# Softmax denominators: an early and a late division for the last sequence, and reciprocals cut in four

## The chip, the cores and the metric

The kernel runs on one core of one Trainium2 chip. The metric is device time in microseconds (us) for one execution; the time of a version is the median of several runs. Before the change it is 2147.88 us (three runs, 2146.33 to 2148.32).

## What is computed

Four layers act in turn on two sequences of 1024 tokens with 512 features, each on a layer-normalised input and each added to its input: a gated recurrence, a feed-forward block with ternary weights, a causal attention, and the same feed-forward block again. The change lies in the attention. Cut to what matters:

```python
q = jnp.concatenate([q1, q2], axis=1)        # two query sets, 16 heads of 32 each
scores = jnp.einsum('bhqd,bhkd->bhqk', q, repeat(k, 2)) * scale
p = jax.nn.softmax(where(causal, scores, min), axis=-1)
y = jnp.einsum('bhqk,bhkd->bhqd', p, repeat(v, 2))
y1, y2 = (y[:, :H], y[:, H:])
y = y1 - sigmoid(x @ Wlam) * y2              # per token and head
out = y.reshape(B, T, D) @ Wo
```

So each of the 32 query heads has a softmax denominator per token. The second set is also weighted by lambda before it is subtracted.

## The kernel before

**Staging.** Each layer keeps its tokens in on-chip memory (`xres`, 16 tiles of 128 tokens). In the attention, a sequence has 16 "pairs": a pair is two heads of one query set that are worked together, and the 32 pairs of both sequences (`pairs`, tuples of sequence `b`, group `g`, position `p`, parity `par`) run one after the other. Each pair has six steps. A step computes two blocks of transposed scores (`weights_step`: `t` products at L866 and L874, exponentials on ScalarE at L882, a causal select on GpSimd at L885 for diagonal blocks), the row maxima of the *next* pair (`maxima_step`: `s` products at L805, reductions on VectorE at L815 and L820), and the products with the values of the *previous* step (`weigh`, L904).

**Numerators and denominators.** The values carry a column of ones, so each product `y` holds 32 rows of numerators and one row of denominators per head. `qb` is the half of the sequence (512 queries). When a half of a pair is complete, ScalarE copies `y` to `ys` (L921) and four transfers on SyncE's queue bring it to its place: two to `share` (L924, the numerators) and two to `tot` (L929, one row of denominators each). `tot` is one tile of 48 rows by 1024 tokens for a sequence: rows 0 to 15 for the first query set, rows 32 to 47 for the second; it is filled with 1.0 first (L917).

**Division.** `divide(b, e)` works on half `e` of `tot`, in place. VectorE takes the reciprocal (L937), multiplies the second set's rows by lambda (L939), and splits the result into a rounded part (L943) and the rest (L944) in a tile `factors`, which GpSimd has cleared (L941). `combine(b, c, e)` spreads the factors of one quarter `c` of the features over the partitions with two products (`r`, L951), multiplies the shares by them on VectorE (L954), and subtracts the second share from the first on GpSimd (L955). `project_out(b, j)` multiplies 128 tokens with `Wo` (L965: eight instructions of TensorE) and VectorE adds the result to the residual (L970). A token tile needs all four quarters of its half. The 16 rows of denominators of quarter `c` come from the four pairs whose `2 * (g % 2) + par` is `c`; for `c = 3` the last of them is the very last pair.

**Order.** TensorE's order in this layer is the program's (`manual_schedule` for PE). The order of the other engines, and of SyncE's queue, is made by the framework's planner, which works with its own idea of costs. In the end part VectorE's order is by hand too. Work beside the pairs is hung on a pair and a step by `at(n, step, f, ...)`, and is issued after that step's `weigh`. For the first sequence, both divisions and all combines hang on pair 16, the first one of the second sequence, whose step 0 also holds the eight value projections (L702). For the second sequence, `divide(1, 0)` hangs on step 3 of the last pair (31), two combines on its step 5, and the rest follows the loop. Steps 0 to 2 of pair 31 also prepare the next layer's first input (L136, L127, L474, L475).

**Room.** All products of this layer go through a ring of seven PSUM banks (`ring_bank`); the `y` and the very last `project_out` have one bank of their own (`edge_bank`). The feed-forward layer that follows loads its 16 weight tiles (`w`, L569) into the room that this layer's tiles leave, in order, from SyncE's queue.

## Time and profile before

| what | value |
|---|---|
| median of 3 runs | 2147.88 us (2146.33 to 2148.32) |
| profiled execution, its own time | 2146.65 us |
| span of that execution, first to last instruction | 2144.9 us |
| mean granted clock of TensorE | 0.996 of full |
| attention layer, roughly | 770 to 1775 us |
| end of it: last pair's step 0 to the next layer's first product | 1720.5 to 1774.6 us |
| reciprocal of half a `tot` (48x512) | 3345 ns, 4 times |
| lambda multiply / cast / subtraction of it | 682 / 418 / 686 ns (medians) |
| `r` product, `b_out` product, `share` multiply, `share` subtraction | 397 / 592 / 682 / 1268 ns (medians) |

How to read it: the page gives busy time by engine over the whole span, but the layers have different limits, so the stretch around a division has to be looked at by itself. A timeline row has the start, the busy time, the engine, the line and the operation (out <- in), the count of instructions merged in it, and in brackets the idle time just before it with what ended it. A wait that no other engine needs is harmless. Matmul durations overlap their neighbours', so a group's length is read from start to start. Dates are us from the start of the span.

### The profile page before, as it was taken

What the parts mean: (1) busy time and instruction counts of PE and PEld (TensorE: products, weight loads), DVE (VectorE), ACT (ScalarE), POOL (GpSimd) and SP (SyncE); (2) the same over time, 40 slices, a digit from 0 to 9 for tenths busy, and PEclk for the clock granted to TensorE, in tenths of its full rate; (3) what the DMA queues carried; (4) which work ended last, traced back from release to release, by engine and by line L of the source; (5) the groups of instructions that cost most, each with busy time, mean ns of one, the idle gap of its engine ahead of it and who ended that gap; (6) DMA issues with size and microseconds to landing.
All of it is one profiled execution on the core that took longest, in us unless ns stands there. A gap on an engine that the chain in (4) does not pass through costs nothing.

```text
span 2144.9 us, 28054 instructions
## 1 busy us (share of the span) xinstructions
PE 2108.8 (98%) x10615; PEld 1242.2 (58%) x10624; DVE 1069.1 (50%) x2272; ACT 835.2 (39%) x1590; POOL 449.8 (21%) x812
## 2 busy tenths in 40 slices
PE   8999999999999999999999999999999999999998
PEld 3444444688888854444444444444545447888887
DVE  5766686533343234555555465464546662433322
ACT  4444333234344322444444422243434523333333
POOL 1312212122122221111111113021212221121212
PEclk9999999999999999999999999999999999999999
DMA  6111211600000111111110101201110033000000
GB/s 255 59 59 62 86 59 74 250 1 1 1 1 1 35 46 37 41 26 41 23 44 21 46 8 37 57 20 42 24 32 15 14 111 132 20 1 20 1 20 20
DMA packets 50999, 98.71 MB, mean 46 GB/s; under 512 B 10800, under 2 KB 19120, under 8 KB 50864
## 3 DMA queue, kind: packets, MB, share of 16 engines
q1 hardware_dynamic: 50864, 96.93, 13.8%
q8 instruction: 83, 1.36, 0.3%
q14 instruction: 52, 0.43, 0.1%
HBM read 58.75 MB, written 16.78 MB: 35 GB/s over the span
## 4 chain that ended last, share of the span: by engine, by line
PE 83%; DVE 8%; DMA 4%; ACT 2%; issue 1%; POOL 1%; SPq 1%; DVEq 0%; ACTq 0%; POOLq 0%
PE y L904 12%; PE g L524 11%; PE u L524 11%; PE f_out L545 11%; PE s L805 10%; PE pq L737 8%; PE t L866 8%; PE pv L702 3%; PE b_out L965 2%; DMA w<-in_w_pt_dram 1%; DMA w_kept<-w 1%; DVE one L174 1%; PE kv L269 1%; DVE w L179 1%; PE ag L269 1%
## 5 line engine op out<-in xcount | busy, mean ns | idle before, releaser
L882 ACT ACTIVATE pr<-t 128x512 f32<-128x512 f32 (+3 forms) x768 | 314.8, 497 | 380.6 <-PE t L874 380.4
L815 DVE CUSTOM_DVE_ANT_0 s<-s,causal 128x128 f32<-128x128 f32 (+3 forms) x512 | 245.3, 510 | 126.1 <-PE s L805 117.4
L904 PE MATMUL y<-pr,val 128*64 128x512 f32 (+3 forms) x1536 | 291.6, 501 | 0.2 <-POOL pr L885 0.2
L539 POOL TENSOR_TENSOR ssq<-ssq,sq 128x512 f32<-128x512 f32 x120 | 155.9, 1299 | 603.6 <-ACT sq L538 603.6
L530 DVE TENSOR_TENSOR h<-h,u 128x512 f32<-128x512 f32 x128 | 88.0, 688 | 362.0 <-PE u L524 355.9
L524 PE MATMUL g<-xs,w 128*128 128x512 f32 x1024 | 262.4, 398 | 0.9 <-ACT xs L474 0.7
L545 PE MATMUL f_out<-w,hs 128*128 128x512 f32 x1024 | 257.7, 394 | 0.3 <-DVE hs L533 0.3
L820 DVE TENSOR_REDUCE nmax<-s 128x1 f32<-128x512 f32 x256 | 165.0, 686 | 184.4 <-PE s L805 184.3
L524 PE MATMUL u<-xs,w 128*128 128x512 f32 x1024 | 256.4, 392 | 0.0
L805 PE MATMUL s<-gr,gr 32*128 32x512 f32 (+3 forms) x1536 | 248.8, 492 | 2.6 <-DVE nmax L815 2.6
L524 PEld LDWEIGHTS u<-xs,w 128*128 128x128 f32 x1024 | 192.4, 188 | 43.5
L545 PEld LDWEIGHTS f_out<-w,hs 128*128 128x128 f32 x1024 | 191.6, 188 | 43.9 <-DVE hs L533 1.1
L524 PEld LDWEIGHTS g<-xs,w 128*128 128x128 f32 x1024 | 190.9, 189 | 44.0 <-ACT xs L474 0.9
L866 PE MATMUL t<-gr,gr 32*128 32x512 f32 (+3 forms) x1536 | 198.8, 533 | 0.0
L904 PEld LDWEIGHTS y<-pr,val 128*64 128x64 f32 x1536 | 93.5, 136 | 179.9 <-issue 105.7
L737 PE MATMUL pq<-b_xt,w_qk 128*128 128x512 f32 x384 | 176.0, 603 | 0.0
L805 PEld LDWEIGHTS s<-gr,gr 32*128 32x128 f32 x1536 | 147.6, 185 | 46.8 <-issue 14.0
L532 ACT CAST hs<-h 128x512 fp32r<-128x512 f32 x128 | 79.4, 621 | 236.6 <-DVE h L530 236.6
L885 POOL TENSOR_SCALAR_AFFINE_SELECT pr<-pr 128x256 f32<-128x256 f32 x256 | 101.3, 408 | 332.2 <-ACT pr L882 332.2
L529 ACT ACTIVATE h<-g 128x512 f32<-128x512 f32 x128 | 76.5, 598 | 224.3 <-PE g L524 224.1
L533 DVE TENSOR_TENSOR hs<-h,hs 128x512 fp32r<-128x512 f32 x128 | 88.6, 692 | 83.1 <-ACT hs L532 83.1
L737 PEld LDWEIGHTS pq<-b_xt,w_qk 128*128 128x128 f32 x384 | 69.6, 189 | 88.0 <-issue 74.0
(155 smaller groups left out, 2211.0 us busy)
## 6 DMA issues: line engine op xcount, KB each, us to landing
w<-w_kept SPq DMA_DIRECT2D x32, 768.0 KB, 8.7
w_kept<-w SPq DMA_DIRECT2D x16, 768.0 KB, 3.2
gr<-gr SPq DMA_DIRECT2D x96, 128.0 KB, 2.3
w<-in_w_gu_dram SPq DMA_DIRECT2D x32, 256.0 KB, 2.8
share<-ys SPq DMA_DIRECT2D x128, 64.0 KB, 2.0
w_in<-in_w_in_t_dram SPq DMA_DIRECT2D x5, 1024.0 KB, 11.2
x<-in_x_dram SPq DMA_DIRECT2D x16, 256.0 KB, 7.1
w<-in_w_pt_dram SPq DMA_DIRECT2D x16, 256.0 KB, 3.5
```

Source lines behind the costliest of these rows:

```text
L524: nc.tensor.matmul(po, ws[f][:, part, ts(k, P)], xs[:, e, k, :], start=(k == 0 and e == 0), stop=(k == NKC - 1 and e == 1),)
L533: nc.vector.tensor_sub(hp[:, 1, :], h, hp[:, 0, :].bitcast(F32))
L539: nc.gpsimd.tensor_add(ssq, ssq, sq)
L545: nc.tensor.matmul(po[j], hp[:, e, ts(j, P)], ws[f][:, 2, :], start=(f == 0 and e == 0), stop=(f == NF - 1 and e == 1),)
L737: nc.tensor.matmul(po, w[:, k, ts(kind, P)], xts[b][:, k, ts(e, BLK)], start=(k == 0), stop=(k == NKC - 1),)
L805: nc.tensor.matmul(part, queries[:, ts(j, P)], keys[:, first : first + nk], start=True, stop=True,)
L815: nc.vector.tensor_tensor_reduce(part, part, causal[:, BLK - part.shape[-1] :], -1.0, 3.0e38, ALU.add, ALU.min, top,)
L820: nc.vector.tensor_reduce(top, part, AX.X, ALU.max, negate=True)
L866: nc.tensor.matmul(banks[u, e][:, :nq], keys[:, ts(kb, P)], queries[:, (qb + 1) * BLK - nq : (qb + 1) * BLK], start=True, stop=False,)
L882: nc.scalar.activation(pr[:, e, :nq], banks[u, e][:, :nq], AF.Exp)
L885: nc.gpsimd.affine_select(out=pr[:, :, :P], in_=pr[:, :, :P], compare_op=ALU.is_ge, fill=0.0, base=0, pattern=[[0, 2], [1, P]], channel_mu ...
L904: nc.tensor.matmul(y[64 * e : 64 * e + 64, lo:], all_values[:, HV * (NH * kb + h) : HV * (NH * kb + h) + 64], pr[:, e, : BLK - lo], start= ...
```

## The change

For the second sequence, the denominators are divided twice. `late_totals` runs in step 0 of the last pair: GpSimd copies `tot` as it is by then (all pairs but the last) to a tile `late_tot`, and clears a tile with room for three sets of factors. The last pair's rows go to `late_tot`. `divide(1, 0)` moves from step 3 to step 0 of that pair and works on `tot`; its factors serve three quarters, whose combines hang on steps 2 and 3. A second division of the first half works on `late_tot`, in step 3, and serves the last quarter, in step 5. The second half is divided from `tot` in step 4, and from `late_tot` in the end part; each set of factors has its own room there. The end part is reordered: `project_out(0)`, three combines of the second half, `project_out` 1 to 3, the last combine, the rest. `late_tot` takes a slot of the tag `w_qk`, the extra factors one of the tag `group0`. Reciprocals of `tot`, the first sequence's too, are taken in four pieces of 128 columns; those of `late_tot` in one.

```diff
@@ weigh
+            tot = held["late"][0] if pair == pairs[-1] else totals[b]
...
-                    out=totals[b][32 * (g // 2) + h : 32 * (g // 2) + h + 1, ts(qb, BLK)],
+                    out=tot[32 * (g // 2) + h : 32 * (g // 2) + h + 1, ts(qb, BLK)],
...
-        def divide(b, e):
-
-            part = totals[b][:, ts(e, BLK)]
-            nc.vector.reciprocal(part, part)
+        def divide(b, e, late=None, to=None):
+
+            part = (totals[b] if late is None else late)[:, ts(e, BLK)]
+            if late is None:
+
+                for i in range(NKC):
+                    nc.vector.reciprocal(part[:, ts(i, P)], part[:, ts(i, P)])
+            else:
+                nc.vector.reciprocal(part, part)
             second = part[rows_of[1]]
             nc.vector.tensor_mul(second, second, lams[b][rows_of[1], ts(e, BLK)])
-            factors[b, e] = b_c.tile([96 + NH, BLK], F32R, tag="factors", name=f"factors{b}_{e}")
-            nc.gpsimd.memset(factors[b, e].bitcast(F32), 0.0)
-            hi, lo = (factors[b, e][64 * i : 64 * i + 32 + NH] for i in range(2))
+            if to is None:
+                to = b_c.tile([96 + NH, BLK], F32R, tag="factors", name=f"factors{b}_{e}")
+                nc.gpsimd.memset(to.bitcast(F32), 0.0)
+            factors[b, e] = to
+            hi, lo = (to[64 * i : 64 * i + 32 + NH] for i in range(2))
             nc.vector.tensor_copy(hi, part)
             nc.vector.tensor_sub(lo, part, hi.bitcast(F32))
+
+        def late_totals(b):
+
+            sums = b_b.tile([32 + NH, SEQ], F32, tag="w_qk", name=f"late_tot{b}")
+            nc.gpsimd.tensor_copy(sums, totals[b])
+
+            more = b_d.tile([96 + NH, 3, BLK], F32R, tag="group0", name=f"factors{b}_late", bufs=2)
+            nc.gpsimd.memset(more.bitcast(F32), 0.0)
+            return sums, [more[:, i, :] for i in range(3)]
...
-        at(n, 3, divide, 1, 0)
-        for c in range(2):
-            at(n, 5, combine, 1, c, 0)
+
+        at(n, 0, lambda: hold("late", late_totals, 1))
+        at(n, 0, divide, 1, 0)
+        for c in range(NKC - 1):
+            at(n, 2 + c // 2, combine, 1, c, 0)
+
+        at(n, 3, lambda: divide(1, 0, held["late"][0], held["late"][1][0]))
+        at(n, 4, lambda: divide(1, 1, None, held["late"][1][1]))
+        at(n, 5, combine, 1, NKC - 1, 0)
...
-        for c in range(2, NKC):
-            combine(1, c, 0)
         ordered.enter_context(tc.manual_schedule(engines={mybir.EngineType.DVE}))
-        divide(1, 1)
-        for j in range(QB - 1):
-            project_out(1, j, held["o", 1])
-        for c in range(NKC):
-            combine(1, c, 1)
-        for j in range(QB - 1, NQ):
-
-            project_out(1, j, held["o", 1], ring_bank if j < NQ - 1 else edge_bank)
+        w_o = held["o", 1]
+        for j in range(QB):
+            project_out(1, j, w_o)
+            if j == 0:
+                for c in range(NKC - 1):
+                    combine(1, c, 1)
+                divide(1, 1, held["late"][0], held["late"][1][2])
+        combine(1, NKC - 1, 1)
+        for j in range(QB, NQ - 1):
+            project_out(1, j, w_o)
+
+        project_out(1, NQ - 1, w_o, edge_bank)
         ordered.close()
```

More of the change, by code (lines that the diff above doesn't have):

```diff
@@ L682 @@
         ]
-        groups, nmax, lams, totals, shares, factors = {}, {}, {}, {}, {}, {}
+        groups, nmax, lams, totals, shares, factors, held = {}, {}, {}, {}, {}, {}, {}
         def load_weights(b, g):
@@ L977, in at @@
             beside.setdefault((n, step), []).append((f, args))
-        held = {}
         def hold(key, f, *args):
```

## The prediction, made before the result was known

> **What bounds the kernel now.** I read the page first, then the list of waits with TensorE as the waiter, then timelines by engine around its longest waits, then the granted clock by the microsecond.

> ```profile
> PE 2108.8 (98%) x10615; PEld 1242.2 (58%) x10624; DVE 1069.1 (50%) x2272; ACT 835.2 (39%) x1590; POOL 449.8 (21%) x812
> ```

> TensorE is busy for 98% of the span. A gain has to come out of its 36 us of gaps, or out of its clock. The waits of TensorE over the whole run:

> ```profile
> PE s L805 <- DVE nmax L815: 2.6, 1, 2.6
> ...
> PE r L951 <- DVE factors L944: 1.8, 1, 1.8
> ...
> PE b_out L965 <- POOL share L955: 0.6, 1, 0.6
> ```

> These three are all that the change can remove; the other long ones lie in the first layer and at block edges. The first (VectorE's timeline, then TensorE's):

> ```profile
> 1251.86 0.14 DVE L815 DVE_READ_ACCUMULATOR2_ANT nmax<- 128x1 f32 x1
> 1252.99 3.35 DVE L937 RECIPROCAL tot<-tot 48x512 f32<-48x512 f32 x1 [0.99 <-DMA tot<-ys]
> 1256.27 0.40 DVE L815 CUSTOM_DVE_ANT_0 s<-s,causal 128x256 f32<-128x256 f32 x1
> ```

> ```profile
> 1257.54 1.51 PE L805 MATMUL s<-gr,gr 32*128 32x384 f32 x8 [2.59 <-DVE nmax L815]
> 1258.98 3.44 PE L904 MATMUL y<-pr,val 128*64 128x512 f32 x8
> ```

> VectorE runs the first sequence's division ahead of maxima whose banks TensorE wants back. TensorE stands 2.59 us, and the y group behind it takes 3.44 us where the same form took 1.94 at 1251.14. The windows say why (columns: stretch, length, PE, PEld, DVE, ACT, POOL, granted clock, DMA):

> ```profile
> 1257.50:1259.00 1.50, 1.46 (x10) 1.04 (x10) 1.43 (x4) 0.00 (x0) 1.29 (x4) 1.00 0.00 0
> ...
> 1260.00:1261.00 1.00, 1.00 (x4) 0.24 (x2) 0.98 (x2) 0.00 (x0) 0.26 (x1) 0.50 0.00 0
> ```

> After the gap the clock is halved, from 1259.3 to 1262.7. That costs 1.50 on y and 0.13 on the transposes behind it: 1.6 us. This place is worth 2.6 + 1.6 = 4.2 us.

> The last pair of heads, TensorE and then VectorE:

> ```profile
> 1729.15 0.66 PE L136 MATMUL xnt_f<-ident,xn_f 128*128 128x128 f32 x4
> 1729.74 1.14 PE L866 MATMUL t<-gr,gr 32*128 32x512 f32 x8
> ...
> 1736.84 1.73 PE L904 MATMUL y<-pr,val 128*64 128x512 f32 x8
> 1740.32 1.19 PE L951 MATMUL r<-factors,head_of 112*128 112x512 f32 x4 [1.75 <-DVE factors L944]
> ```

> ```profile
> 1734.99 3.35 DVE L937 RECIPROCAL tot<-tot 48x512 f32<-48x512 f32 x1 [2.74 <-DMA tot<-ys]
> ```

> Here the 1.75 us are those of the division that waits for this pair's own sums; the clock stays whole. Steps 0 to 2 of this pair are over by 1729.74. Keep that date.

> **The change part by part.**

> *Reciprocals in four pieces.* A 48x512 reciprocal is 3.345 us, the 128x8 one 0.203, the 128x4 ones 0.17 to 0.18 and the 128x1 one 0.136: about 6.3 ns a column and 0.13 fixed. A piece of 128 columns is then about 0.94 us, four are 3.75, 0.4 more than one. [...] I go by the rows: with one piece before the maxima, the first of the two wanted banks comes back about 0.94 + 2 x 0.38 = 1.7 us after 1253.0, at 1254.7, and TensorE asks for it at about 1254.95. The gap goes, and the half clock with it: -4.0 (leaving 0.2 of the 4.2). Bounds: -4.2, and +0.4 if the four stay together. The second reciprocal of this sequence (1273.5) lies beside value projections where VectorE waits 2.7 us for each; nothing there.

> *The early division in the last pair.* It is placed in step 0 and waits for more than it needs. The pool copy of the sums reads all of the tile, so also what pair 30 wrote last; and the reciprocal writes in place, so it waits for the copy. Dates from before: the last of those four sum and share transfers is issued at 1726.08 and lands some 1.9 later (1733.04 to 1734.99 is the nearest like it): 1728.0. Copy 48x1024 on GpSimd: not in the trace. Below: its memset of that shape, 0.97. Above: twice a two-input 128x512, 2.5. Nearest are the one-input selects, 0.41 for 256 and 0.735 for 512, which make 1.4 for 1024; I take 1.3. So 1729.3. Then four pieces 3.75, multiply 0.72, cast 0.42, subtraction 0.69: 5.6; with some of the 0.69 of an xs subtraction that comes ready at 1731.5, the factors are there at about 1735.4 (1734.7 to 1737.5). GpSimd's memsets (1536 columns, about 1.4 by the 0.95 of 1024; and 0.52) end by 1731.3, ahead of the cast. They and the copy block the queue, but nothing in it is due between 1726.1 and 1735.6.

> *Three combines moved to steps 2 and 3.* TensorE goes in program order. The first r product stands right behind the transposes at 1729.15, so it is due at 1729.74 and gets its factors at 1735.4: a new gap of 5.65 us (4.9 to 7.7). Behind it in TensorE's queue stand steps 3 to 5 and everything after. The first sequence has the same spacing of steps, but there 27.7 us of value projections lie in step 0; here nothing does. [...]

> *The late division, first half.* Sums still land at 1735.0, since the y they come from precede the new gap. VectorE then holds the four multiplies (4 x 0.68), reciprocal 3.35, 0.72, 0.42, 0.69, and two more multiplies: 9.3 us from 1735.4, to about 1744.7. TensorE reaches its combine at 1735.4 + 1.2 (four r) + 3.2 + 0.6 + 3.1 + 2.5 = 1746.0, later still at half clock. So 1.75 goes. In a bad order (the 5.6 us of the other early division first) it is up to 4 late again.

> *The second half's two divisions and the reordered end.* The early one is 5.6 us of VectorE before the combines behind project_out(0), due at about 1746.0 + 0.6 + 0.9 + 3.5 = 1751; VectorE's whole list ends at about 1735.4 + 16 = 1751.4. The late one needs about 4.2 us from the y copy to the landing (1742.39 to 1746.57 before) and 5.2 of work; it lies beside project_out 1 to 3, 3 x 3.45 = 10.4 us of TensorE. Vector additions queue behind it, whose banks are wanted much later. Only the last combine's multiplies and GpSimd subtraction (0.4 + 1.36 + 1.27 = 3.0) against six of the eight products of project_out(4) (2.6) may show 0.4. The 0.62 of before goes: project_out(0) now has the y products as well. Together I put 0.5 for waits in this order (0 to 4).

> *Room.* The copy of the sums lies in the weights' room, where a load of the next layer will land, so that load and those behind it on SP's queue wait until the late division has read. Before, five loads went at 1745.5, two at 1757.7 and nine at 1775.2. Some may slip by about 10 us; the fifth is wanted about 22 us after that layer's start (5.6 us a step). Zero, unless slips exceed 20 us.

> **Sum.** Last pair: + 5.65 + 1.6 + 0.5 - 1.75 - 0.62 = + 5.4. First sequence: - 4.0. Net about + 1.5 us (1.4, rounded). The profiled execution took 2146.65 (span 2144.9, 1.75 around it), so 2148.1; it lies 1.2 under the median 2147.88, and against that median I say 2149.4. A measurement here tells about 0.2%, 4.3 us, from no change.

> **Rivals.**

> *A, as summed*, 0.6: 2149.4, own range 2146 to 2152.5.

> *B, the pieces run back to back*, 0.25, the slower side. The planner that orders VectorE put the whole reciprocal ahead of the maxima once; if in its reckoning VectorE is idle for longer than two pieces, they still stand together, at 1253. Price: the 4.0 isn't earned and 0.4 is added, 2147.9 + 5.4 + 0.4 = 2153.7. It decides from the third piece on, when the bank is about 1.9 us late. For it: VectorE had waited 0.99 us for the sums' transfer there, so the planner believed it idle. Against: the maxima's products were done at 1251.2.

> *C, the change does both things freely*, 0.05: no new gap, and all three waits go: 4.2 + 1.75 + 0.6, some 6.5 less, 2141.4. It needs factors at 1729.74, only 1.7 after the landing, against 6.9 of work.

> *D, order on VectorE or GpSimd*, 0.1: the 3.35 us late reciprocal slips in ahead of the multiplies that free banks, or the pool copy ahead of step 1's selects (due 1725.4, 2.6 before the landing): 2 to 4 more than A, 2152.4.

> Range: 2146.0 to 2154.4, which takes in B and most of D. Faster by over 0.2%: C, 0.05. Slower: most of B, some of D and of A's upper end, 0.3. Within: 0.65.

> **What would show it.** In the profile after: 48x128 reciprocals with 0.9 each; no wait of s on nmax near 1255 and clock 1.00 there; in the last pair a wait of r for factors of about 5.6 us followed by a clock of 0.5; the late division's factors ready before their r. No such wait there would refute me, and so would four adjacent pieces at 1253.

## The result, and the profile after

The changed kernel takes 2160.92 us (four runs, 2157.49 to 2162.71) beside 2147.57 of before: 1.0061 times as long, 95% interval 1.0043 to 1.0078. The forecast was 2149.4, at most 2154.4. The profiled execution took 2162.71, span 2161.0: 16 us more than before. I place them by four marks that both traces have: the first product of the first feed-forward layer, the first value projection (`pv`) of the second sequence, the first input transpose (`xnt_f`) of the last pair, and the first product of the feed-forward layer behind the attention:

| stretch | before | after | difference |
|---|---|---|---|
| start to the first feed-forward product | 398.6 | 402.3 | +3.7 |
| from there to the first `pv`, with the first sequence's division | 870.4 | 872.4 | +1.9 |
| `pv` to the last pair's `xnt_f` | 453.8 | 454.1 | +0.4 |
| `xnt_f` to the next layer's first product ("the tail") | 51.8 | 61.9 | +10.0 |
| rest, to the last instruction | 370.3 | 370.3 | 0.0 |

Nothing in the first stretch was edited; the runs below show that it is chance. The busy times, the first line of the page after, say little: VectorE has 10 us more for 20 instructions more, and TensorE 10 us more for the same 10615 products: a product at half clock counts as busy for longer (a `y` group takes 3.44 us in the prediction's rows where 1.94 is its time at whole clock).

```profile
PE 2118.6 (98%) x10615; PEld 1246.7 (58%) x10624; DVE 1079.4 (50%) x2292; ACT 835.5 (39%) x1590; POOL 451.7 (21%) x813
```

The list of TensorE's waits over the whole run, after, tells more. Columns: who waits for whom, us in total, times, the longest.

```profile
PE r L968 <- DVE factors L952: 6.8, 1, 6.8
...
PE a_out L421 <- POOL yt L395: 2.9, 1, 2.9
...
PE y L904 <- POOL pr L885: 1.9, 2, 1.7
PE t L866 <- DVE nmax L820: 1.1, 1, 1.1
...
PE s L805 <- DVE nmax L815: 0.6, 2, 0.4
```

The 2.59 us of `s` are down to 0.6 in two waits, the 1.75 of `r` has become 6.8, and two waits are new: `t` for a maximum, and `y` for one of GpSimd's selects (1.65). (`a_out` is of the first layer.)

**First sequence.** VectorE's timeline after, then TensorE's:

```profile
1257.71 0.95 DVE L941 RECIPROCAL tot<-tot 48x128 f32<-48x128 f32 x1 [1.00 <-DMA tot<-ys]
...
1260.06 2.56 DVE L941 RECIPROCAL tot<-tot 48x128 f32<-48x128 f32 x3
1262.65 0.68 DVE L945 TENSOR_TENSOR tot<-tot,lam 16x512 f32<-16x512 f32 x1
1263.37 0.42 DVE L951 CAST factors<-tot 48x512 fp32r<-48x512 f32 x1
1263.82 0.69 DVE L952 TENSOR_TENSOR factors<-tot,factors 48x512 fp32r<-48x512 f32 x1
1264.54 0.69 DVE L820 TENSOR_REDUCE nmax<-s 128x1 f32<-128x512 f32 x1
```

```profile
1259.86 1.51 PE L805 MATMUL s<-gr,gr 32*128 32x384 f32 x8 [0.20 <-DVE nmax L815]
...
1265.29 0.37 PE L866 MATMUL t<-gr,gr 32*128 32x128 f32 x1 [1.08 <-DVE nmax L820]
...
1266.21 2.31 PE L805 MATMUL s<-gr,gr 32*128 32x512 f32 x6 [0.38 <-DVE nmax L815]
1268.44 3.11 PE L904 MATMUL y<-pr,val 128*64 128x512 f32 x8
```

One piece stands ahead of step 3's maxima, and there only 0.20 us of wait is left, as forecast. But the other three pieces, the lambda multiply, the cast and the subtraction follow in one row, 4.5 us to 1264.54, ahead of the next step's maximum. The wait has moved on by one step, and the half clock (1268.6 to 1272.1) with it: `y` takes 3.11 us, as it took 3.44 before.

**Last pair.** TensorE after, then VectorE, then GpSimd:

```profile
1735.17 0.66 PE L136 MATMUL xnt_f<-ident,xn_f 128*128 128x128 f32 x4
1742.61 2.05 PE L968 MATMUL r<-factors,head_of 112*128 112x512 f32 x4 [6.78 <-DVE factors L952]
1744.59 2.19 PE L866 MATMUL t<-gr,gr 32*128 32x512 f32 x8
...
1756.23 2.79 PE L904 MATMUL y<-pr,val 128*64 128x512 f32 x8 [1.65 <-POOL pr L885]
```

```profile
1734.93 4.19 DVE L941 RECIPROCAL tot<-tot 48x128 f32<-48x128 f32 x5 [0.27 <-POOL late_tot L957]
...
1740.81 0.94 DVE L941 RECIPROCAL tot<-tot 48x128 f32<-48x128 f32 x1
1741.78 0.68 DVE L952 TENSOR_TENSOR factors<-tot,factors 48x512 fp32r<-48x512 f32 x1
...
1746.51 3.34 DVE L943 RECIPROCAL late_tot<-late_tot 48x512 f32<-48x512 f32 x1
...
1752.69 1.29 DVE L971 TENSOR_TENSOR share<-share,r 128x512 f32<-128x512 f32 x2
```

```profile
1733.87 1.03 POOL L957 COPY late_tot<-tot 48x1024 f32<-48x1024 f32 x1 [1.72 <-DMA tot<-ys]
...
1754.06 1.76 POOL L972 TENSOR_TENSOR share<-share,share 128x512 f32<-128x512 f32 x1 [6.08 <-DVE share L971]
1755.78 1.48 POOL L885 TENSOR_SCALAR_AFFINE_SELECT pr<-pr 128x256 f32<-128x256 f32 x4
```

The reciprocal row counts five pieces, not four: the fifth, and one more at 1740.81, belong to the second half's early division and stand ahead of the factors that TensorE waits for (the run `no_slip` below takes them away). Later the 3.34 us late reciprocal and the rest of the second half's division hold the multiplies of quarter 2 until 1752.69; GpSimd's queue has the subtraction of that quarter ahead of four selects, and `y` waits for those. The clock, by windows (columns as in the prediction's):

```profile
1740.00:1742.00 2.00, 0.00 (x0) 0.00 (x0) 1.97 (x4) 0.00 (x0) 0.00 (x0) 0.50 0.01 1
...
1744.00:1746.00 2.00, 2.00 (x10) 1.05 (x12) 2.00 (x5) 0.00 (x0) 0.53 (x1) 0.50 0.00 0
...
1747.00:1748.00 1.00, 1.00 (x6) 0.40 (x8) 1.00 (x1) 1.00 (x3) 0.98 (x1) 1.00 0.00 0
...
1758.00:1760.00 2.00, 2.00 (x6) 0.50 (x2) 0.21 (x1) 0.00 (x0) 0.00 (x0) 0.50 0.00 0
```

It is halved twice, from 1739.7 to 1746.5 and from 1756.7 to 1760.2. TensorE works in the last 3.9 us of the first stretch and all 3.4 of the second. I put the loss at half of that, 3.65 us, an estimate from the eight `t` at 1744.59, which take 2.19 us where the eight at 1733.08 take 1.14. The waits are 6.78 + 1.65 + 0.45 (`b_out`) where they were 1.75 + 0.62: 6.5 more. Together 10.2, against 10.0 measured.

### The profile page after: what moved, and what is told of

The parts are those of the page before. It is cut to its first block, busy times and chain, and to the rows that moved or that the text cites. A ratio compares the mean times of both kernels' runs of the same rounds, so it can differ in the third digit from the quotient of the medians.

```text
span 2161.0 us, 28078 instructions
## 1 busy us (share of the span) xinstructions
PE 2118.6 (98%) x10615; PEld 1246.7 (58%) x10624; DVE 1079.4 (50%) x2292; ACT 835.5 (39%) x1590; POOL 451.7 (21%) x813
## 3 DMA queue, kind: packets, MB, share of 16 engines
q8 instruction: 83, 1.36, 0.3%
## 4 chain that ended last, share of the span: by engine, by line
PE 81%; DVE 10%; DMA 3%; ACT 2%; POOL 1%; issue 1%; SPq 0%; DVEq 0%; ACTq 0%; POOLq 0%
PE y L904 12%; PE g L524 11%; PE u L524 11%; PE f_out L545 11%; PE s L805 10%; PE pq L737 8%; PE t L866 8%; PE pv L702 3%; PE b_out L982 2%; DMA w<-in_w_pt_dram 2%; DMA w_kept<-w 2%; DVE one L174 1%; PE a_out L421 1%; DVE w L179 1%; PE mt L845 1%
## 5 line engine op out<-in xcount | busy, mean ns | idle before, releaser
L815 DVE CUSTOM_DVE_ANT_0 s<-s,causal 128x128 f32<-128x128 f32 (+3 forms) x512 | 245.3, 510 | 126.0 <-PE s L805 117.3
L904 PE MATMUL y<-pr,val 128*64 128x512 f32 (+3 forms) x1536 | 292.6, 502 | 1.9 <-POOL pr L885 1.9
L805 PE MATMUL s<-gr,gr 32*128 32x512 f32 (+3 forms) x1536 | 250.1, 492 | 0.6 <-DVE nmax L815 0.6
L866 PE MATMUL t<-gr,gr 32*128 32x512 f32 (+3 forms) x1536 | 201.6, 536 | 1.2 <-DVE nmax L820 1.1
L904 PEld LDWEIGHTS y<-pr,val 128*64 128x64 f32 x1536 | 93.7, 136 | 182.3 <-issue 108.7
L805 PEld LDWEIGHTS s<-gr,gr 32*128 32x128 f32 x1536 | 147.9, 185 | 46.0 <-issue 14.0
L866 PEld LDWEIGHTS t<-gr,gr 32*128 32x128 f32 x1536 | 68.6, 184 | 90.8 <-issue 54.2
```

The lines of the kernel that those rows point to most:

```text
L805: nc.tensor.matmul(part, queries[:, ts(j, P)], keys[:, first : first + nk], start=True, stop=True,)
L815: nc.vector.tensor_tensor_reduce(part, part, causal[:, BLK - part.shape[-1] :], -1.0, 3.0e38, ALU.add, ALU.min, top,)
L866: nc.tensor.matmul(banks[u, e][:, :nq], keys[:, ts(kb, P)], queries[:, (qb + 1) * BLK - nq : (qb + 1) * BLK], start=True, stop=False,)
L904: nc.tensor.matmul(y[64 * e : 64 * e + 64, lo:], all_values[:, HV * (NH * kb + h) : HV * (NH * kb + h) + 64], pr[:, e, : BLK - lo], start= ...
```

## The experiments

All times are medians; ratios are to runs of the kernel before on the same chip. "Tail" and "`pv`" are the stretches of the table above, of the profiled execution.

**The same kernel again** (`after_again`).

> The changed kernel once more. The profiled one lost 16.1 us of span: 4.5 by the end of the first layer, whose code is not touched, 1.5 at the first sequence's division, 10.1 in the last pair and the end part. Theory (the 4.5 are the luck of the clock's windows): runs of this same program differ by some us, the profile taken now may show an offset near 0 at 1200 us, and the median lies 11 to 16 above before. Rival (the 4.5 belong to the program): every run has them, the offset at 1200 us is 4.5 again and the median 15 to 16 above before.

2158.14 us, ratio 1.0045 (1.0032 to 1.0058). To the first feed-forward product it takes 397.6 us where the first profile took 402.3; tail +8.5. So the first layer's share was chance. In the 14 profiled executions of this study that first stretch runs from 396.2 to 402.3 us, with code that no version touches.

**First sequence's reciprocals in pieces, alone** (`pieces_first`).

```diff
-            nc.vector.reciprocal(part, part)
+            if b == 0:
+                for i in range(NKC):
+                    nc.vector.reciprocal(part[:, ts(i, P)], part[:, ts(i, P)])
+            else:
+                nc.vector.reciprocal(part, part)
```

> The kernel before with the first sequence's reciprocals alone in four pieces. Theory (three of the four pieces, and the rest of the division, stand ahead of the next step's maxima; the gap moves one step on and the clock still halves): 0 to +2 us against before, a wait of the t or s products of about 1.5 us near 1264, clock 0.5 behind it. Rival (the prediction's): -4.0 us, no gap.

2149.12, ratio 1.0005 (0.9996 to 1.0013): nothing gained. VectorE's order is that of the changed kernel, one piece, four maxima, three pieces and the rest. The stretch to `pv` is 0.9 us longer than before.

**Last sequence's change, alone** (`last_seq_only`: the changed kernel, with the edit above turned round: whole reciprocals for the first sequence).

> The changed kernel with the first sequence's reciprocals whole, so only the last sequence's part of the change. Theory: +10 us against before from the wait at step 2 of the last pair (6.8), its half clock (about 2 lost), a second wait for a select (1.7) with a half clock (1.7 lost), less the two old waits (2.4); the place at 1253 as before. Rival (the pieces of the first sequence or a reordering elsewhere carry part of it): under +8.

2157.54, ratio 1.0049 (1.0036 to 1.0061); to `pv` +0.1, tail +10.0. The loss is the last sequence's.

**The first sequence's loss by order alone** (`div_behind`). The whole reciprocal, not cut, is queued on VectorE behind the first copy of the value projections.

```diff
-                    at(n + 1, 1, divide, b, 0)
+                    at(n + 1, 1, divide_behind, b, 0)
...
+        def divide_behind(b, e):
+
+            with tc.issue_after(held["pv0"].ins):
+                divide(b, e)
```

> The kernel before, with the first half's division of the first sequence queued on VectorE behind the first copy of value products, in one piece. Theory (the first sequence's loss is VectorE's order alone): the 2.6 us gap at 1255 and the half clock behind it go, -4.2 us against before. Rival (the gap only moves, or the clock's loss is made up elsewhere): 0 to -2.

2141.16, ratio 0.9972 (0.9961 to 0.9983): faster, and by more than expected. VectorE's timeline of this kernel, then TensorE's:

```profile
1265.24 0.69 DVE L705 COPY val<-pv 128x512 f32<-128x512 f32 x1 [2.73 <-PE pv L702]
1265.85 3.33 DVE L941 RECIPROCAL tot<-tot 48x512 f32<-48x512 f32 x1
```

```profile
1252.13 1.02 PE L809 MATMUL s<-gr,gr 32*128 32x384 f32 x8
1253.09 1.94 PE L908 MATMUL y<-pr,val 128*64 128x512 f32 x8
```

The same `s` stand without a wait, the `y` behind them takes its 1.94 us at whole clock, and the stretch to `pv` is 5.4 us shorter.

**Combines two steps later** (`combines_later`; this run and the next three change `last_seq_only`).

```diff
-            at(n, 2 + c // 2, combine, 1, c, 0)
+            at(n, 4 + c // 2, combine, 1, c, 0)
```

> The kernel with only the last sequence changed, but its three combines of the first half hang on steps 4 and 5 of the last pair instead of 2 and 3. Theory (the loss is that the r products stand in TensorE's queue before their factors can be there): the 6.8 us wait of r for factors at step 2 goes, with its half clock, since the factors are ready about 5 us before step 4's r products; what is left is a shorter wait for the last quarter's factors or for the second half. Its last part is 5 to 9 us shorter than with the combines in steps 2 and 3, the time about 2149 to 2152. Rival (the second division of each half is too much work for VectorE in this pair, wherever the combines stand): the wait shows up again at the later combines or in the end part with nearly its size, and the time stays at 2155 to 2158.

2158.12, ratio 1.0042 (1.0029 to 1.0054); tail +8.4. The rival was right. TensorE's timeline of this kernel, then VectorE's:

```profile
1746.86 2.07 PE L968 MATMUL r<-factors_late,head_of 112*128 112x512 f32 x4 [7.68 <-DVE factors_late L952]
```

```profile
1730.55 4.19 DVE L941 RECIPROCAL tot<-tot 48x128 f32<-48x128 f32 x5 [0.28 <-POOL late_tot L957]
...
1740.58 3.35 DVE L943 RECIPROCAL late_tot<-late_tot 48x512 f32<-48x512 f32 x1
...
1746.12 0.69 DVE L952 TENSOR_TENSOR factors_late<-late_tot,factors_late 48x512 fp32r<-48x512 f32 x1
```

Three divisions (first half early and late, second half early) and one `xs` subtraction of 0.69 fill VectorE from 1730.55 to 1746.81 without a break. Whichever product asks first waits for what is left of those 16 us. No room on TensorE's side helps; the work has to start earlier, or not be done.

**No pieces ahead of the factors** (`no_slip`). The second half's early division is queued behind the first half's.

```diff
+        def second_half():
+            with tc.issue_after(held["early"].ins):
+                divide(1, 1, None, held["late"][1][1])
...
+        at(n, 4, second_half)
```

> The kernel with only the last sequence changed; the second half's early division is queued on VectorE behind the subtraction that ends the first half's early one, so its pieces can't slip in before it. Theory: the wait of r at step 2 was 6.8 us where 5.65 was worked out because two pieces of 0.94 us stood in front of the factors; without them it is about 4.9 to 5.7 us, and the time is 1 to 2.5 us less, about 2155.5. Rival (the wait is set by GpSimd's copy and clears, not by those pieces): the wait stays at 6.8 us and the time at 2157.5.

2153.11, ratio 1.0024 (1.0015 to 1.0034). TensorE's timeline of this kernel:

```profile
1738.06 2.05 PE L968 MATMUL r<-factors,head_of 112*128 112x512 f32 x4 [4.52 <-DVE factors L952]
```

The wait falls to 4.5 us, and the tail to +4.7, more than expected: the wait of `y` for the selects behind the subtraction goes too, though GpSimd's queue has the same order. (The 0.25 us of another `y` for a select, earlier in the pair, stands in the kernel before as well.) The multiplies of quarter 2 now end at 1747.36, and TensorE comes to that `y` only at 1749.8.

**The early division brought forward** (`spread`). Its pieces are written to a place of their own, so that they don't wait for GpSimd's copy, and stand behind maxima of the pair before; the second half's early division comes behind the multiplies of the last quarter.

```diff
+        at(n - 1, 3, early_piece, 0, "top")
+        at(n - 1, 4, early_piece, 1, "top")
+        for i in (2, 3):
+            at(n, 0, early_piece, i, "min")
+        at(n, 0, lambda: divide(1, 0, done=held["room"][:, SEQ:]))
...
-        at(n, 4, lambda: divide(1, 1, None, held["late"][1][1]))
...
+            with tc.issue_after(held["mul"].ins):
+                divide(1, 1, None, held["late"][1][1])
...
         at(n, 5, combine, 1, NKC - 1, 0)
+        at(n, 5, second_half)
```

> The kernel with only the last sequence changed, with the early division brought forward: it no longer waits for GpSimd's copy (its reciprocals are written to another place), and its four pieces stand one by one behind the maxima of the last steps of pair 30 and in step 0 of the last pair; the second half's early division comes after the multiplies of the last quarter. Theory (the loss is all in the wait for factors at step 2 and what follows from it): no wait of r at step 2, no half clock there; the last part is 7 to 9 us shorter than with the early division in step 0, the time 2147 to 2150, about that of before. Rival (two divisions a half cost VectorE, and so TensorE, in any place): the time stays above 2153.

2157.16, ratio 1.0045 (1.0031 to 1.0058): missed. The wait at step 2 is gone, as the theory says, but the tail is still +8.3. TensorE's waits from 1700 to 1780 us in this kernel:

```profile
PE r L972 <- DVE factors_late L956: 3.3, 1, 3.3
PE y L906 <- POOL pr L887: 2.1, 2, 1.8
```

Both come with a half clock (1742.2 to 1745.6, 1752.4 to 1759.2). The 3.3 us are those of the second half's early division. VectorE's timeline shows where it stands:

```profile
1745.11 1.28 DVE L975 TENSOR_TENSOR share<-share,r 128x512 f32<-128x512 f32 x2 [3.01 <-PE r L972]
1746.31 3.37 DVE L945 RECIPROCAL tot<-tot 48x128 f32<-48x128 f32 x4
```

It is queued behind the multiplies of the last quarter, and for these VectorE stood idle for 3.0 us until TensorE had made their `r`. So the wait comes from this place in VectorE's order. The expectation of `first_half_only` below says that there is no idle time before these `r` products; the row shows 3.0 us of it. Whether the pieces would cost nothing there was not tried.

**With the first sequence mended too** (`both_mended`: `spread` with the edit of `div_behind`).

> The kernel of the run before this one (early division of the last sequence brought forward) with, for the first sequence, its whole reciprocal queued on VectorE behind the first copy of the value projections, as in the run div_behind. Theory: the two edits add up; the first sequence's place gives some 5 to 6 us, the last part 0 to 1 us less or more than before, together about 2142 to 2144, faster than before and about as fast as div_behind alone (2141.2), so that an early and a late division bring nothing of their own. Rival (the early and late division do take the waits of 1.75 and 0.62 away once their factors are early): 1.5 to 2.5 us under div_behind, 2139.

2151.19, ratio 1.0012 (1.0005 to 1.0018): missed by as much as the run before. To `pv` 5.0 us less, tail +8.1: the two edits add up, and the last pair's still loses.

**Only the first half divided twice** (`first_half_only`). As in `spread`, but the second half is divided once, from `late_tot`, and the end part has its old order.

```diff
-        for c in range(NKC - 1):
-            at(n, 2 + c // 2, combine, 1, c, 0)
+        for c in range(2):
+            at(n, 1 + c, combine, 1, c, 0)
...
-        at(n, 5, combine, 1, NKC - 1, 0)
-        at(n, 5, second_half)
+        at(n, 5, combine, 1, 2, 0)
```

> Only the first half of the last sequence is divided twice, early (pieces behind the maxima of the pair before) and late; the second half once, as before the change, and the end part stands in the old order. Combines of quarters 0 and 1 hang on steps 1 and 2, quarter 2 on step 5, quarter 3 follows the loop; first sequence as before. Theory (an early division is free where VectorE is idle, between 1715 and 1730, and what cost 3.3 us in the run spread was the second half's early division, which has no idle time before its r products): the wait of 1.75 us for factors goes and none takes its place; from the last pair's first input transposes to the next layer's first product it is about 50.0 us, against 51.8 before and 60.1 in spread; the time is 1 to 2 us under before, about 2146.5. Rival (a division more costs time in any place): that stretch is 54 us or longer and the time over 2150.

2144.94, ratio 0.9992 (0.9984 to 1.0). Tail 49.9 us, 2.0 less than before and within 0.2 of the forecast for it, though not quite for the reason given: a wait of 0.85 us for the late factors is left, and the 0.62 us of `b_out` are gone as well. VectorE's timeline of this kernel shows the early division in the time that was idle:

```profile
1715.53 0.94 DVE L1061 RECIPROCAL late_tot<-tot 48x128 f32<-48x128 f32 x1
...
1719.13 1.75 DVE L1061 RECIPROCAL late_tot<-tot 48x128 f32<-48x128 f32 x2
...
1722.09 0.69 DVE L956 TENSOR_TENSOR factors<-late_tot,factors 48x512 fp32r<-48x512 f32 x1
```

TensorE's timeline of this kernel, at the first `r` of the last quarter:

```profile
1740.13 0.73 PE L972 MATMUL r<-factors_late,head_of 112*128 112x512 f32 x2 [0.85 <-DVE factors_late L956]
```

0.7 us are given back ahead of the tail, at four `s` products in pair 30 right behind the piece of 1715.53: they take 1.54 us where they took 1.05 before.

**Both, and the measure for it** (`first_half_both` is `first_half_only` with the edit of `div_behind`).

> The run before this one, with the first sequence's first division queued on VectorE behind the first copy of the value projections, as in div_behind. Theory: the two add up, about 2139.5, some 1.7 us under div_behind. Rival (the wait of 1.75 us is only moved on to the next wait in that pair): no difference from div_behind.

> The kernel before with only the first sequence's first division queued behind the first copy of the value projections, once more, beside the two runs above. Theory: 2141 again, 0.3% under before; the stretch from the first value projection of the second sequence to the end is as before. No rival; it is the measure for the run before it.

2139.72, ratio 0.9967 (0.9954 to 0.9979), beside 2141.29, ratio 0.9975 (0.9965 to 0.9986), of the one edit alone. The tail is 2.0 us shorter and the stretch before it 0.7 longer; the times don't tell these 1.3 us from nothing. Both versions are faster than the kernel before and than the changed one, and nearly all of it is the order of one reciprocal.

**The pieces, held apart by hand** (`pieces_held`), one behind the last maximum of each step.

```diff
-                    at(n + 1, 1, divide, b, 0)
+                    for i in range(NKC):
+                        at(n + (i == 3), (3 + i) % STEPS, first_piece, b, i)
+                    at(n + 1, 1, divide, b, 0, True)
...
+        def first_piece(b, i):
+            part = totals[b][:, ts(i, P)]
+            with tc.issue_after(held["top"].ins):
+                nc.vector.reciprocal(part, part)
```

> The kernel before with the first sequence's first reciprocal in four pieces, as in pieces_first, but each piece is queued by hand behind the last maximum of a step (steps 3, 4 and 5 of the maxima, then the first of the next pair), and the rest of the division behind the fourth. Theory (pieces help as the prediction said when one at most stands ahead of a step's maxima; in the changed kernel three and the rest of the division stood together): no wait of s for nmax over 0.5 us near 1255 to 1266, clock whole there, and 4 to 5.4 us less than before, about 2142.5. Rival (a piece ahead of the maxima or of the copy of the turned maxima is enough to hold TensorE): a wait of about 1 us with a half clock at one of the later steps, and the time at 2146 to 2149.

2142.97, ratio 0.9979 (0.9972 to 0.9985). VectorE's timeline of this kernel:

```profile
1254.42 0.94 DVE L950 RECIPROCAL tot<-tot 48x128 f32<-48x128 f32 x1
1255.74 0.69 DVE L820 TENSOR_REDUCE nmax<-s 128x1 f32<-128x512 f32 x1 [0.38 <-PE s L805]
...
1258.12 0.94 DVE L950 RECIPROCAL tot<-tot 48x128 f32<-48x128 f32 x1
...
1261.46 0.94 DVE L950 RECIPROCAL tot<-tot 48x128 f32<-48x128 f32 x1
```

No wait of TensorE is listed from 1240 to 1280, and the stretch to `pv` is 4.9 us shorter. (The tail of this profile is 1.5 us longer: there the old wait of 1.75 us was followed by a half clock, and `b_out` waits 1.0 us where it waited 0.62.) The pieces do what the prediction asked of them once their order isn't left to the planner.

## Why the prediction was wrong

The sum was +1.4 us. The medians say +13.4 and, measured again, +10.5; the two places that the sum is about make +10.9 in the first profile.

**The first sequence: -4.0 forecast, +0.9 measured.** The step that failed is "The gap goes, and the half clock with it: -4.0", worked out "with one piece before the maxima". For those maxima it held: wait 0.20, a piece 0.95 us. The sum ended there, though, and never asked where the other three pieces and the 1.8 us behind them would stand. Rival B had the right point, "from the third piece on", but put all four ahead of the same step. The table shows TensorE's time from step 3's transposed products to the next `y`, and from there to `pv`:

| kernel | to `y` | to `pv` |
|---|---|---|
| before | 5.98 | 10.06 |
| after | 3.58 | 13.38 |
| `after_again` | 3.57 | 15.02 |
| `pieces_first` | 3.58 | 13.32 |
| `pieces_held` | 2.14 | 9.13 |
| `div_behind` | 2.14 | 8.41 |

The split gave 2.4 us in the first column and lost 3.3 in the second: +0.9. That compares profiles in which the half clock lasted 3.4 us. Where it lasted 6.8, the changed kernel takes 18.6 us (`after_again`, both columns) and the whole reciprocal 16.9 to 17.2 (`combines_later`, `no_slip`, `spread`): +1.4 to +1.7. The columns also show that the place was worth 5.5 us, not 4.2. Besides the wait of 2.59 and the 1.6 of the clock there are 1.3 us more: 0.5 lie in the eight `s` behind the wait, which take 1.51 us where they take 1.02 in `div_behind`: their weight loads start at 1257.54 and 1257.92, and VectorE's last two maxima end at 1257.48 and 1257.86, so the two banks come back 0.38 us apart; the rest is not taken apart.

**The last pair, +5.4 forecast, +10.0 and +8.5 measured.** The main mechanism was right: a wait of `r` at step 2, with the date of the landing (1728.0 forecast, 1727.9 after moving the row of 1733.87 back by the 6.0 us that this pair started later) and the price of the copy (1.3, measured 1.03) nearly right. The sizes of its terms were off, and one wait stood in none of them:
- The wait, 5.65: measured 6.78. Two pieces of 0.94 us of the other early division stood ahead of the factors; I had priced such a slip for the late factors alone. Without them (`no_slip`) it is 4.5, less than 5.65 because the four pieces in a row take 3.38 us where I had 3.75, the copy is shorter, and the `xs` subtraction falls behind the factors; and the whole tail is then +4.7, beside the +5.4 of the sum. That this is so near is in part luck: the shorter wait is made up for by a half clock of 6.8 us (1737.3 to 1744.1), twice as long as the one that the 1.6 was read from.
- The half clock, 1.6: that is the price read at the 2.59 us wait of the first sequence; that a half clock would go with the 5.65 us wait was my estimate, and no trace of before shows one in this pair. It came, from 1739.7 to 1746.5. By the estimate above it cost 1.95 at this wait, and a second one, from 1756.7 to 1760.2, cost 1.7.
- "Waits in this order", 0.5: measured 1.65 for `y`. I had costed VectorE's list as ending in time (1751.4) and looked at who waits for its factors, not at who waits for its multiplies: a GpSimd subtraction with four selects behind it. Rival D had the order right (the late reciprocal slips in ahead of multiplies), but named banks as what TensorE would lack. This wait stands in the traces of four kernels (1.7 to 1.8 us; 0.7 in the changed kernel's second profile), and not in `no_slip`, where those multiplies are early; the queue's order wasn't tried by itself.
- Removed waits, -1.75 and -0.62: the first did go; of the second 0.45 stayed.

What a second division costs depends on where it stands in VectorE's order, as `combines_later`, `spread` and `first_half_only` show: 0.7 us when it is spread over the time from 1712 to 1723, in a stretch where VectorE was busy for 8.3 of 15 us before (1715 to 1730), but a wait of 3.3 to 7.7 us where TensorE asks for its factors while VectorE is still at it. That both halves can't be divided twice at a gain is not shown: `spread` tried one place for the second half, with idle time of VectorE just ahead of it. The room for the copy cost nothing, as forecast: the last stretch is 370.3 us in all kernels.

**The rest of the profiled difference: +3.7 in the first layer, +1.0 ahead of the first division and +0.4 behind `pv`.** The first is chance, and the 1.0 too: from the first feed-forward product to step 3's transposed products of that division the traces take 854.2 to 854.5 us where a half clock lasts 3.4 us behind that first product (seven profiles, before among them), 854.7 to 854.9 where it lasts 4.6 to 5.1 us (five, `after_again` among them), and 855.3 and 855.4 where it lasts 6.0 and 6.2 (`combines_later`, after). The 0.4 stands in all four profiles of kernels with pieces in the first sequence, and not in `last_seq_only`; how it comes about stays open.

## What to carry to other kernels

Cutting a long instruction in pieces helped here only once the order of the pieces was fixed: look for what stands behind the first piece, and behind the last one, and who needs what is queued there. Before adding work to an engine to take a wait away, count its list from the earliest moment its data are there to the moment its result is due; if the list is longer than that stretch, the wait moves on but doesn't get shorter. Moving one reciprocal out of the way gave 0.25 to 0.28% here, more than all the added divisions (the best of them took 1.3 us from the profile).
